# Projecting the queries and keys of head pairs two and three inside the softmax of the pair ahead, in a Mamba and attention hybrid

## The chip, the cores and the metric

The kernel runs as one program on one core of a Trainium2 chip. The metric is the device time of one execution in microseconds (us), the median of three runs. Engines are named as in the profile: PE is TensorE (its weight loads are PEld), DVE is VectorE, ACT is ScalarE, POOL is GpSimd, SP is SyncE, which here only issues DMAs. L725 is line 725 of the kernel before.

## The reference: what is computed

The input holds 8 images of 384 channels and 32 by 32 positions, that is 8 batches of 1024 tokens with 384 channels, all float32. Two layers follow each other for each batch.

Layer 0 norms the channels and runs a Mamba block forward and backward over the tokens: a state of 16 numbers per channel and direction is carried by `h = dA * h + dBu`, and `y = sum over n of h * C`. A depthwise 3x3 convolution is added, and the residual.

Layer 1 is a transformer layer. What matters here is its attention, with 6 heads of 64 channels:

```python
t = x + attention(layernorm(x)); t = t + ffn(layernorm(t))
...
qkv = x @ Wqkv
q, k, v = jnp.split(qkv, 3, axis=2)
...
scores = jnp.einsum('bhqd,bhkd->bhqk', q, k)      # causal mask
attn = jax.nn.softmax(scores, axis=-1)
out = jnp.einsum('bhqk,bhkd->bhqd', attn, v)
return out @ Wproj + bproj
```

The feed-forward layer (384 to 1536 to 384) quantizes by the largest magnitude in groups of batches. It can touch only the first 5 batches, so the kernel computes it for those alone.

## The kernel before: tiles, stages and the order of the work

**Layout.** Channels lie on the 128 partitions in NC = 3 chunks, tokens along the free axis in NH = 2 halves of HB = 512. A head pair is one chunk of 128 channels: head e of pair c sits on partitions 64e to 64e+63.

**Three streams share the engines.** *Before the scan* (`before_scan`): norm, input projection, convolutions, gates, step sizes. *The scan*: 768 units (`units`), each of 2 states of one chunk and half. A unit is a multiply on POOL (`s_first`, L588), two exponentials on ACT (L601), two scans on DVE (L606), a second multiply on POOL (L612), and 8 transposes on PE that add into one PSUM bank (L620). *After the scan*: `attention` and, for five batches, `feed_forward`.

**Who sets the order.** Each stage emits a list of steps, each with a planned cost (2.5 us where none is given). `spread_over` merges lists in proportion to these costs. The end of the kernel function lays all attention and feed-forward steps in a row (`rest`), and deals the scan's slots between them so that a batch's units come before its attention (`due`). Functions are then called in that order. The framework's scheduler turns the calls into one instruction stream per engine: an earlier call has priority, but an instruction whose input or buffer isn't ready at its planned time lets later ones pass. `pin` keeps marked instructions in program order, and `at_once` moves the second head's matmul next to the first head's. [...]

**Attention of one batch** (`attention`, L674):

1. Load the gated scan output, project it (`op`, L695), add to `t`; layernorm of `t`.
2. Project queries and keys, L713 to L732: s = 0 for q and 1 for k, m the head pair, h the token half. Each of these 12 steps takes a PSUM bank, three matmuls of 512 columns (each is two PE instructions in the trace, so 6), and a copy to `q` or `k` by `nc.any`, that is on ACT or DVE, whichever the scheduler finds free.
3. Project the values, 8 steps (L743), then make tile `o`.
4. For each head pair c and query half g, `probabilities` gives one step for each 128 queries and each 512 keys: one score matmul for each head into a bank of tag `s` (L786), mask, row maximum and shift on DVE (L800), exponential with row sum on ACT (L810). There are 12 such steps a pair. `weighted_values`, one half behind, transposes the probabilities on PE (L862), copies them (ACT, L864) and multiplies by the values (L875).
5. Output projection (`ap`, L934).

The last batch's attention runs after all scans, with nothing beside it.

**PSUM.** There are 8 banks, tagged `y` 1, `da` 2, `s` 2, `pt` 2, `av` 1. `bank(name)` without a tag takes `s` and `pt` in turn, so the projections of queries, keys and values rotate over four banks. `s` also serves the scores, `pt` the transposes.

**SBUF.** The pool `big` has six buffers of 128 x 3072 numbers. In attention `t` (normed input), `gy`, `wqk` (weights), `q`, `k`, `v` and `o` come from it. `gy` is free after step 1; in the kernel before, `t` and `wqk` are free after step 3.

Of the kernel before, what the change touches and what calls it, by code (L numbers as in the profile page):

```python
# [20 lines left out]
NC = C // P  # L21
# [33 lines left out]
def kernel(  # L55
# [31 lines left out]
    def btile(name):  # L87
        return big.tile([P, NC, L], F32, name=name, tag="big")
# [10 lines left out]
    def bank(name, tag=None):  # L99
        if tag is None:  # L100
            turn[0] += 1
            tag = ("s", "pt")[turn[0] % 2]
        return ps.tile([P, HB], F32, name=name, tag=tag, bufs=BANKS[tag])

    def half(h):
        return slice(h * HB, (h + 1) * HB)
# [173 lines left out]
    def layernorm(src, name, emit):  # L280

        dst = src
        st = {}
        for h in range(NH):

            @emit.of(6.0)
            def _(h=h):
                mean = mean_of(lambda c: src()[:, c, half(h)], f"mean_{name}_{h}")
                for c in range(NC):
                    nc.vector.tensor_tensor(  # L290
                        dst()[:, c, half(h)], src()[:, c, half(h)], mean, ALU.subtract
                    )
                st[h] = squares(dst(), h, name)

        for h in range(NH):

            @emit.of(6.0)
            def _(h=h):
                var = mean_of(lambda c: st[h][c], f"var_{name}_{h}")
                rstd_of(var, 1)  # L300
                for c in range(NC):
                    nc.vector.tensor_tensor(  # L302
                        dst()[:, c, half(h)], dst()[:, c, half(h)], var, ALU.mult
                    )
# [369 lines left out]
    def attention(b, emit_ffn, emit):  # L674
        st = {}

        @emit
        def _():

            st["t"] = btile(f"t_{b}")  # L680
            st["gy"] = btile(f"gy_{b}")
            for h in range(NH):
                for c in range(NC):
                    load(st["gy"][:, c, half(h)], spilled[b, "gy", c, h])
            for c in range(NC):
                load(st["t"][:, c, :], spilled[b, "t", c])
# [24 lines left out]

        layernorm(lambda: st["t"], f"na_{b}", emit)

        for s in range(2):
            for m in range(NC):
                for h in range(NH):

                    @emit
                    def _(s=s, m=m, h=h):
                        if m == 0 and h == 0:  # L720
                            st["qk"[s]] = btile(f"{'qk'[s]}_{b}")
                        qp = bank(f"qp_{b}_{s}_{m}_{h}")
                        for c in range(NC):
                            o = s * C + m * P
                            nc.tensor.matmul(  # L725
                                out=qp,
                                lhsT=st["wqk"][:, c, o : o + P],
                                rhs=st["xn"][:, c, half(h)],
                                start=(c == 0),
                                stop=(c == NC - 1),  # L730
                            )
                        nc.any.tensor_copy(st["qk"[s]][:, m, half(h)], qp)  # L732
# [176 lines left out]

        waiting = Steps()  # L910
        for c in range(NC):
            for g in range(NH):
                made = Steps()
                probabilities(c, g, made)
                emit.extend(spread_over(made, waiting))
                waiting = Steps()
                weighted_values(c, g, waiting)
        emit.extend(waiting)

        feeds = b < FFN_B  # L920
# [162 lines left out]
    def spread_over(*lists):  # L1083

        keyed = []
        for k, steps in enumerate(lists):
            total, at = sum(us for _, us in steps), 0.0
            for f, us in steps:
                keyed.append(((at + us / 2) / total, k, (f, us)))
                at += us  # L1090
        return [e[2] for e in sorted(keyed, key=lambda e: e[:2])]
# [57 lines left out]
    for i, b in enumerate(ORDER):  # L1149
        if i > 0:  # L1150
            due.append((sum(us for _, us in rest), i * per))
        fed = Steps()
        rest += steps_of(attention, b, fed) if i < B - 1 else []
        if fed and later:
            fed = spread_over(fed, steps_of(before_scan, later.pop(0), ("pt", "pt", "av")))
            fed = [(f, JOINT * us) for f, us in fed]
        rest += fed
# [11 lines left out]
    for _, _, f in sorted(timed, key=lambda e: e[:2]):  # L1169
        f()  # L1170
    run(steps_of(attention, ORDER[-1], Steps()))


# [49 lines left out]
```

## Time and profile before

| | us |
|---|---|
| median of 3 runs (5047.65 to 5053.58) | 5047.94 |
| profiled execution, its own time | 5051.18 |
| its span, first to last instruction | 5049.4 |
| POOL busy / PE busy (modelled) | 3691.4 / 4101.8 |
| DVE busy / ACT busy | 3599.9 / 2721.4 |

In the trace the eight blocks of query and key projections begin at 868, 1550, 2219, 2913, 3611, 3956, 4314 and 4868 us. The first scores of the same attentions follow at 924, 1610, 2284, 2984, 3673, 4013, 4373 and 4915 us, and the last score matmuls begin at 1113, 1800, 2489, 3173, 3864, 4219, 4557 and 5013 us. The last attention starts its first matmul at 4840 us, when POOL has no more work.

How to read it: a group line gives line, engine, operation, what it writes and reads with shapes, count, then busy time, mean ns of one, and the idle time of the engine before it with what ended it. A window line gives a stretch of time and each engine's busy time in it with the number of instructions, then the granted PE clock. A wait line gives who waited for whom, total us, times, longest us. Matmuls are pipelined and their ends are modelled, so the distance between their starts tells more of PE's load than their durations.

### The profile page before, as it was taken

The page shows a single profiled execution, that of the slowest core. Times are in us where ns is not written, and L with a number is a line of the kernel's source. Part 1 is how long each engine was busy: PE and PEld are TensorE (multiplying, and loading weights), DVE is VectorE, ACT ScalarE, POOL GpSimd, SP SyncE. Part 2 cuts the span into 40 slices and gives each one's busy share as a digit, 9 for nine tenths or more (in the row PEclk, how much of TensorE's full clock was granted, in tenths as well). Part 3 has the DMA queues.
Part 4 walks back from the last instruction along what each step waited for, and adds up shares of the span by engine and source line. Part 5 has one row for each costly group of instructions (what it writes and reads, how often), then busy time and mean ns, then how long its engine had stood idle before and what let it go on. Part 6 is the DMA issues. An engine that isn't in the chain of part 4 may idle for free. (4 is left out here: it accounts for less than half of the span.)

```text
span 5049.4 us, 50760 instructions
## 1 busy us (share of the span) xinstructions
PE 4101.8 (81%) x16458; PEld 2191.0 (43%) x16458; DVE 3599.9 (71%) x4780; ACT 2721.4 (54%) x4891; POOL 3691.4 (73%) x1944
## 2 busy tenths in 40 slices
PE   4687787878788888788787888888888978878899
PEld 1243343544434444444443444434444544444444
DVE  6887978667786777876678867678767666666523
ACT  4565665565645656545556446565365455464426
POOL 0578687987669886778876788768788978877710
PEclk7788797989889899888998889898888989989999
DMA  6554646324363334453234633335543334324210
GB/s 230 197 176 158 207 156 226 113 86 144 135 210 117 115 114 163 156 174 125 103 129 143 208 109 127 114 116 191 174 131 115 104 99 141 106 92 132 89 64 26
DMA packets 365010, 696.36 MB, mean 138 GB/s; under 512 B 30104, under 2 KB 88904, under 8 KB 364744
## 3 DMA queue, kind: packets, MB, share of 16 engines
q1 hardware_dynamic: 355232, 676.97, 39.7%
q10 hardware_dynamic: 9512, 16.15, 0.9%
q8 instruction: 130, 2.13, 0.2%
q14 instruction: 136, 1.11, 0.1%
HBM read 527.33 MB, written 165.68 MB: 137 GB/s over the span
## 5 line engine op out<-in xcount | busy, mean ns | idle before, releaser
L588 POOL TENSOR_TENSOR g<-ud,bc 128x1024 f32<-128x1024 f32 x768 | 1839.3, 2395 | 652.0 <-PE y L620 513.1
L612 POOL TENSOR_TENSOR g<-g,bc 128x1024 f32<-128x1024 f32 x768 | 1820.5, 2371 | 228.4 <-DVE g L606 175.6
L601 ACT ACTIVATE da<-dl,amat 128x512 f32<-128x512 f32 x1536 | 1056.1, 691 | 1481.1 <-DVE g L606 1438.6
L606 DVE TENSOR_TENSOR_SCAN g<-da,carry,g 128x512 f32<-128x512 f32 x768 | 957.6, 1271 | 405.7 <-POOL g L588 364.7
L606 DVE TENSOR_TENSOR_SCAN g<-da,g 128x512 f32<-128x512 f32 x768 | 906.4, 1210 | 472.7 <-POOL g L588 439.9
L620 PE MATMUL y<-ident,g 128*128 128x128 f32 x6144 | 932.4, 299 | 270.7 <-POOL g L612 214.6
L620 PEld LDWEIGHTS y<-ident,g 128*128 128x128 f32 x6144 | 772.5, 154 | 729.1 <-POOL g L612 339.9
L786 PE MATMUL s<-k,q 64*128 64x512 f32 (+3 forms) x1152 | 405.1, 610 | 122.9 <-DVE nm L800 111.5
L800 DVE CUSTOM_DVE_ANT_0 pr<-s,cmask 128x512 f32<-128x512 f32 (+3 forms) x576 | 300.6, 545 | 212.6 <-PE s L786 185.8
L810 ACT ACTIVATE pr<-pr,nm 128x512 f32<-128x512 f32 (+3 forms) x576 | 348.8, 606 | 141.7 <-DVE nm L800 139.5
L862 PE MATMUL pt<-ident,pr 128*128 128x128 f32 x1728 | 301.9, 305 | 73.5 <-ACT ptn L864 32.9
L993 PE MATMUL hp<-t,w 128*128 128x512 f32 x720 | 339.4, 617 | 27.1 <-DMA w<-w1s 15.2
L1038 PE MATMUL yp<-h,w 128*128 128x512 f32 x720 | 329.2, 615 | 10.3 <-DMA w<-w2s 5.5
L341 PE MATMUL in<-xn,win 128*128 128x512 f32 x576 | 293.3, 651 | 46.3 <-DVE xc L463 14.8
L862 PEld LDWEIGHTS pt<-ident,pr 128*128 128x128 f32 x1728 | 209.1, 153 | 237.2 <-ACT ptn L864 88.6
L875 PE MATMUL av<-ptn,v 128*64 128x512 f32 (+3 forms) x1152 | 276.6, 563 | 23.9 <-DVE o L889 16.2
L864 ACT COPY ptn<-pt 128x512 f32<-128x512 f32 (+3 forms) x576 | 255.2, 474 | 74.0 <-PE pt L862 72.6
L725 PE MATMUL qp<-t,wqk 128*128 128x512 f32 x576 | 263.9, 608 | 17.5 <-DVE t L302 12.0
L400 DVE SCALAR_TENSOR_TENSOR loc<-xn,vec,loc 128x496 f32<-128x496 f32 (+3 forms) x384 | 260.4, 721 | 24.2 <-ACT loc L389 22.7
L611 POOL COPY carry<-g 128x2 f32<-128x2 f32 x384 | 85.8, 224 | 248.1 <-DVE g L606 248.1
L786 PEld LDWEIGHTS s<-k,q 64*128 64x128 f32 x1152 | 138.4, 208 | 251.8 <-DVE nm L800 187.6
L1038 PEld LDWEIGHTS yp<-h,w 128*128 128x128 f32 x720 | 140.3, 199 | 178.9 <-issue 166.3
(155 smaller groups left out, 4809.8 us busy)
## 6 DMA issues: line engine op xcount, KB each, us to landing
bc<-rows SPq DMA_DIRECT2D x512, 512.0 KB, 4.1
dl<-sdl SPq DMA_DIRECT2D x160, 256.0 KB, 2.9
ud<-sud SPq DMA_DIRECT2D x160, 256.0 KB, 2.7
t<-st SPq DMA_DIRECT2D x63, 512.0 KB, 5.3
su<-u SPq DMA_DIRECT2D x48, 512.0 KB, 3.8
du<-su SPq DMA_DIRECT2D x96, 256.0 KB, 4.5
sdl<-du SPq DMA_DIRECT2D x96, 256.0 KB, 2.4
sud<-du SPq DMA_DIRECT2D x96, 256.0 KB, 2.8
```

Source lines behind the costliest of these rows:

```text
L341: nc.tensor.matmul(out=mp, lhsT=st["win", c][:, k, i, :], rhs=st["xn"][:, k, half(h)], start=(k == 0), stop=(k == NC - 1),)
L588: pin(nc.gpsimd.tensor_tensor(g, ud, sst["bc", 0, u.b, u.part, u.n], ALU.mult))
L601: nc.scalar.activation(da, sst["dl", u.b, u.c, u.part], AF.Exp, scale=amat[:, u.c, n : n + 1])
L606: nc.vector.tensor_tensor_scan(gi[:, ::step], da[:, ::step], gi[:, ::step], first, ALU.mult, ALU.add)
L612: pin(nc.gpsimd.tensor_tensor(g, g, sst["bc", 1, u.b, u.part, u.n], ALU.mult))
L620: nc.tensor.matmul(out=y[:, j, :], lhsT=g[:, i, chunk(j)], rhs=ident, is_transpose=True, start=(u.opens and i == 0 and j == 0), stop=(u.cl ...
L786: mm = nc.tensor.matmul(out=ss[e][:, : k1 - k0], lhsT=st["q"][rows_of(e), c, chunk(qi)], rhs=st["k"][rows_of(e), c, k0:k1], start=True, st ...
L800: nc.vector.tensor_tensor_reduce(out=x, in0=ss[e][:, :w], in1=mask, scale=-1.0, scalar=-MASKED, op0=ALU.add, op1=ALU.min, accum_out=m,)
L810: nc.scalar.activation(x, x, AF.Exp, bias=m, scale=-1.0, accum_out=rs[:, i, e, kb : kb + 1])
L862: nc.tensor.transpose(pt[:, chunk(i)], pr[:, e, chunk(j % QT)], ident)
L993: nc.tensor.matmul(out=hp, lhsT=st["w1"][:, c, chunk(m % 2)], rhs=st["xn"][:, c, half(h)], start=(c == 0), stop=(c == NC - 1),)
L1038: nc.tensor.matmul(out=yp, lhsT=st["w2", k // 6][:, k % 6, :], rhs=st["h", k // NC][:, k % NC, half(h)], start=(k == 0), stop=(k == NF - 1),)
```

## The change

The step list of the query and key projections is split by head pair. Those of pair 0 are emitted where they were. Those of pairs 1 and 2 (8 of the 12 steps) go to lists of their own, and `spread_over` deals the list of pair c+1 evenly among the softmax steps of pair c. Their order among themselves stays: q of both halves, then k of both halves. Steps of pairs 1 and 2 take their PSUM bank from tag `s` alone instead of from `s` and `pt` in turn. Number, size and planned cost of all steps stay as they were.

```diff
+        qk_of = [emit] + [Steps() for m in range(1, NC)]
         for s in range(2):
             for m in range(NC):
                 for h in range(NH):
 
-                    @emit
+                    @qk_of[m]
                     def _(s=s, m=m, h=h):
                         if m == 0 and h == 0:
                             st["qk"[s]] = btile(f"{'qk'[s]}_{b}")
-                        qp = bank(f"qp_{b}_{s}_{m}_{h}")
+                        qp = bank(f"qp_{b}_{s}_{m}_{h}", None if m == 0 else "s")
...
         waiting = Steps()
         for c in range(NC):
+            pair = []
             for g in range(NH):
                 made = Steps()
                 probabilities(c, g, made)
-                emit.extend(spread_over(made, waiting))
+                pair.extend(spread_over(made, waiting))
                 waiting = Steps()
                 weighted_values(c, g, waiting)
+            emit.extend(spread_over(pair, qk_of[c + 1]) if c + 1 < NC else pair)
         emit.extend(waiting)
```

## The prediction, made before the changed kernel ran

> **What bounds the kernel now.** I read the page first, then busy time by stage, then the waits inside one softmax stretch, then the order of time in single steps.
>
> ```profile
> PE 4101.8 (81%) x16458; PEld 2191.0 (43%) x16458; DVE 3599.9 (71%) x4780; ACT 2721.4 (54%) x4891; POOL 3691.4 (73%) x1944
> ...
> L588 POOL TENSOR_TENSOR g<-ud,bc 128x1024 f32<-128x1024 f32 x768 | 1839.3, 2395 | 652.0 <-PE y L620 513.1
> L612 POOL TENSOR_TENSOR g<-g,bc 128x1024 f32<-128x1024 f32 x768 | 1820.5, 2371 | 228.4 <-DVE g L606 175.6
> ...
> L725 PE MATMUL qp<-t,wqk 128*128 128x512 f32 x576 | 263.9, 608 | 17.5 <-DVE t L302 12.0
> ```
>
> No engine is full over the whole span. A scan unit costs POOL 2.395 + 2.371 = 4.77 us, and no unit can pass faster. L725 has 576 instructions: 8 attentions x 12 steps x 6. The stages, three projection blocks first, then the softmax that follows each (busy us of PE, PEld, DVE, ACT, POOL, each with its instruction count, then the granted PE clock):
>
> ```profile
> 868.00:904.00 36.00, 36.00 (x124) 18.73 (x123) 22.61 (x24) 13.74 (x22) 34.81 (x22) 1.00 0.17 50
> 3611.00:3652.00 41.00, 37.71 (x120) 19.06 (x119) 24.67 (x26) 13.89 (x22) 33.84 (x15) 0.96 0.31 103
> 4868.00:4899.00 31.00, 31.00 (x74) 13.75 (x73) 3.15 (x6) 7.69 (x13) 0.00 (x0) 1.00 0.00 0
> ```
> ```profile
> 924.00:1113.00 189.00, 151.51 (x816) 85.62 (x814) 134.96 (x239) 119.32 (x282) 167.44 (x83) 0.87 0.30 103
> 3673.00:3864.00 191.00, 158.93 (x840) 90.10 (x840) 133.41 (x238) 119.81 (x282) 167.70 (x95) 0.86 0.36 117
> 4915.00:5013.00 98.00, 92.55 (x532) 45.06 (x532) 44.52 (x165) 71.85 (x205) 0.00 (x0) 1.00 0.00 1
> ```
>
> Over the seven attentions that have scans beside them, blocks last 36, 38, 45, 48, 41, 36 and 39 us, 283 in sum with POOL busy 257.6 (91%). The softmax stretches last 1354 us with POOL busy 1160.2 (85.7%). So POOL is near its bound in both, a little nearer in the blocks. The last attention has no scans: there its own chain counts alone.
>
> PE is full in the blocks: in the last one 72 instructions start within 30.9 us, 0.43 us apart, a step being 6 x 0.43 = 2.58 us. In softmax, PE only looks full. Where I subtract from the distances between matmul starts what each needs (0.43 us for 512 columns, 0.107 for 128), 77 to 94 of each 184 to 206 us are left over, and 27 of the 117 us of the last attention's (4915 to 5032). The waits within the stretch from 3673 to 3864 us:
>
> ```profile
> DVE g L606 <- POOL g L588: 33.2, 21, 3.4
> POOL g L588 <- PE y L620: 21.4, 12, 3.6
> PEld s L786 <- DVE nm L800: 21.3, 23, 2.8
> ...
> PE s L786 <- DVE nm L800: 12.5, 10, 2.0
> ```
>
> PE waits above all for DVE to empty a score bank, and POOL then waits for transposes queued on PE behind that. In order of time, on PE:
>
> ```profile
> 3707.42 1.09 PE L620 MATMUL y<-ident,g 128*128 128x128 f32 x8
> ...
> 3716.30 0.47 PE L862 MATMUL pt<-ident,pr 128*128 128x128 f32 x1 [2.84 <-ACT ptn L864]
> 3716.56 1.91 PE L620 MATMUL y<-ident,g 128*128 128x128 f32 x8
> ```
>
> After a hole of 2.84 us the same eight transposes take 1.91 us instead of 1.09. And a score step of the last attention:
>
> ```profile
> 4920.81 1.73 PE L786 MATMUL s<-k,q 64*128 64x512 f32 x4 [0.31 <-DVE nm L800]
> ...
> 4921.97 0.69 DVE L800 CUSTOM_DVE_ANT_0 pr<-s,cmask 128x512 f32<-128x512 f32 x1 [0.60 <-PE s L786]
> ...
> 4922.70 0.64 DVE L800 CUSTOM_DVE_ANT_0 pr<-s,cmask 128x512 f32<-128x512 f32 x1
> ```
>
> Both `s` banks are held from 4920.81 to 4923.34, 2.53 us. From first matmul to end of the second reduction the mean over 36 steps is 2.43 us here, 88 of 99 us; in the stretch at 3673 it is 4.14 us, 149 of 194. So the two `s` banks are the tightest thing in softmax after POOL.
>
> **What the Trainium skill says.** *TensorE: Matmul & The Clock Gate*, section "HAM oscillation — how this bites in real kernels": gaps of several us let the PE clock fall to half, and the next matmuls run cold. The trace agrees: 0.86 granted in softmax against 0.96 to 1.00 in blocks, and 1.91 against 1.09 us. *PSUM — Partial Sum Buffer*, "Engine vs sequencer instructions": matmuls start and complete in program order; so transposes of the scan stand behind a waiting score, as the 21.4 us show. *Perfetto Trace Analysis*, "Matmuls": independent groups should rotate through PSUM banks so that emptying one overlaps the next. The block does so with four banks and PE starts every 0.43 us; with two it is not shown.
>
> **The change, part by part.**
>
> *Removed ahead:* 8 steps an attention. In the last one 8 x 2.58 = 20.6 us, all on the path. In the other seven a step costs 283 / 84 = 3.37 us including the scan work within, so 27.0 us each.
>
> *Added inside:* the same 48 PE instructions and 8 copies (0.58 us on ACT, 0.66 on DVE) an attention. No new instruction and no DMA.
>
> *Last attention.* Each step holds an `s` bank for 2.58 + 0.04 (copy lag here) + 0.59 = 3.2 us. It can start when the first score bank is emptied. Of its 2.58 us, about 0.7 lie beside the second reduction and 0.4 in the 0.33 us a step that banks are free (2.76 us period, 99.3 / 36, less 2.43) and similar holes; about 0.3 come back because the next pair of scores gets its second bank only after the copy. So 2.58 - 1.1 + 0.3 = 1.8 us, x 8 = 14.4, against 20.6 removed: **-6**. Bounds: no more than PE's leftover in pairs 0 and 1 (18.7 us by the same subtraction, 4915 to 4991) can be gained; at the full 3.2 us a step it is 25.6 - 20.6 = +5.
>
> *Seven attentions beside scans.* The planned costs don't change, so the moved time takes its units along: 27.0 x 0.91 = 24.6 us of POOL work. Softmax then has 165.7 + 24.6 = 190.3 us of POOL work on average. At its old share that is 190.3 / 0.857 = 222.1 against 193.4 + 27.0 = 220.4: +1.7. At the blocks' 91% it is 209.1: -11.3. I take 87.2%: PE's 84 us of leftover can take in 20.6, the holes that cool the clock shrink, and a projection step asks little of DVE and ACT (one copy), so scans get through beside it; but holes that are waits for an `s` bank can't be filled by a step that needs one. 190.3 / 0.872 = 218.2: -2.2 each, **-16** for seven. Bounds: -79 and, where the banks decide, +35 (rival one).
>
> *Edits costed at nothing.* `t` and `wqk` stay until pair 1 is nearly through: with `q`, `k`, `v`, `o` all six `big` buffers are taken. The trace shows loads into `big` inside softmax (`t2` at 965 us and `x` at 993 us of the first; the next batch's `gy` at 3721). They would come near the start of pair 2 (1041 and 3797 us there), while first needed at 1117 (`ap`), 1166 (`ms`) and 3913 us (`op`); landing takes 5 to 8 us. Cover gone, it is some 8 us at a load. On SP row loads of the scan queue behind such a wait; SP already waits 20 us at a time for POOL in this stretch. First use of pair c+1's keys comes an eighth of a pair, some 8 us, after their last step: covered.
>
> Sum: -6 - 16 = -22. Against the profiled execution's 5051.2 (span 5049.4 and 1.8 around it) that is 5029. The median of the runs lies 3.2 lower: **5026**.
>
> **Rivals.**
>
> *One: the score banks decide (slower).* Beside scans a copy often starts late: 0.3 to 2.5 us after the last matmul in the blocks. A step holds one of two banks for 2.58 + 1.6 + 0.6 = 4.8 us and the next scores need both. Scores of pairs 0 and 1 hold them 101 of 126 us there. For: 77% held, and PE's commonest wait is this one. Against: the other bank still takes one head. It decides from 3.37 us added a step. At 4.0: 0.63 x 8 x 7 = +35, and +5 at the end: 5088.
>
> *Two: the holes are filled.* Softmax reaches the blocks' 91%: -79, and -14 at the end: 4955. For: PE is idle 43% there. Against: its holes come from the bank waits.
>
> *Three: POOL paces both, nothing moves.* +12 (7 x 1.7) - 6 = +6: 5054. It also stands for the scheduler drawing the projections forward, since their inputs are ready, so that the block stays. Against: `s` banks are soon taken.
>
> **How the numbers follow.** Forecast 0.41, own range 5005 to 5037; rival one 0.26, two 0.16, three 0.17. About 10 us (0.2%) is what a measurement can tell from no change. Faster: 0.35 of the forecast, 0.16 of two, 0.03 of three: 0.54. Same: 0.05 + 0.02 (of one) + 0.10 = 0.17. Slower: 0.01 + 0.24 + 0.04 = 0.29. Range 4962 to 5085: it leaves out about half of two and a third of one.
>
> **What would show it.** Right: blocks of 24 instructions at L725; softmax stretches near 218 us with POOL at 87%; the last attention's pairs 0 and 1 some 14 us longer; PE clock in softmax above 0.87. Wrong: score steps holding their banks over 5 us, L786 waiting more for L732 copies than PE had leftover, or POOL's idle before L588 on `y` grown. A reordered schedule in the feed-forward stages, which the change doesn't touch, would break the sum too.

## The result, and the profile after

The changed kernel is slower. Its median is 5089.14 us (four runs, 5087.84 to 5090.45) against 5050.47 us for the kernel before (four runs, 5047.65 to 5053.58); the ratio is 1.008, with an interval of 1.0068 to 1.0092. The profiled execution took 5087.84 us, its span 5086.1 us: 36.7 us more than the span before.

The page of the changed kernel, the lines that answer to those of before:

```profile
PE 4123.5 (81%) x16458; PEld 2194.2 (43%) x16458; DVE 3600.6 (71%) x4785; ACT 2725.2 (54%) x4886; POOL 3691.2 (73%) x1944
...
L588 POOL TENSOR_TENSOR g<-ud,bc 128x1024 f32<-128x1024 f32 x768 | 1835.8, 2390 | 689.8 <-PE y L620 559.0
L612 POOL TENSOR_TENSOR g<-g,bc 128x1024 f32<-128x1024 f32 x768 | 1820.0, 2370 | 227.0 <-DVE g L606 176.7
...
L727 PE MATMUL qp<-t,wqk 128*128 128x512 f32 x576 | 289.7, 644 | 31.9 <-DVE nm L802 18.4
```

The counts of instructions (but for five that went from ACT to DVE), POOL's busy time and the mean of its two operations have stayed. What has grown is idle time: POOL's ahead of L588 for transposes on PE went from 513.1 to 559.0 us, and the projections (L727) now wait for `nm`, the row maximum of a score step, which they never did before.

By stage, in the changed kernel: three blocks from the first projection of queries to the first score, now with four steps of queries and keys ahead of the values, so not of the same extent as the windows of before (length, busy us of PE, PEld, DVE, ACT and POOL, granted PE clock, DMA share, GB/s).

```profile
867.00:899.00 32.00, 31.94 (x129) 19.26 (x127) 20.62 (x23) 11.94 (x19) 31.52 (x20) 1.00 0.15 50
3644.00:3681.00 37.00, 33.71 (x130) 19.99 (x128) 21.83 (x23) 14.50 (x25) 32.74 (x15) 0.95 0.34 114
4901.00:4927.00 26.00, 26.00 (x74) 13.59 (x72) 2.34 (x4) 7.15 (x14) 0.00 (x0) 1.00 0.00 1
```

And the softmax that follows each, from the first score to the last:

```profile
899.00:1121.00 222.00, 183.22 (x892) 100.41 (x892) 149.50 (x253) 127.96 (x294) 189.44 (x97) 0.87 0.30 104
3681.00:3908.00 227.00, 187.26 (x922) 101.12 (x921) 147.79 (x252) 130.04 (x297) 188.06 (x105) 0.88 0.32 104
4927.00:5050.00 123.00, 117.62 (x579) 54.62 (x578) 45.98 (x165) 76.52 (x214) 0.00 (x0) 1.00 0.00 1
```

The first two softmax stretches lasted 189 and 191 us before; they last 222 and 227 now, with POOL busy 85% and 83%, where it was 89% and 88% before. Summed over the attentions, from the start of each stage's first matmul to the start of the next stage's (softmax: to the start of its last score):

| us, seven attentions beside scans | before | after | POOL busy before | POOL busy after |
|---|---|---|---|---|
| queries and keys, up to the first value projection | 288.4 | 102.1 | 259.2 | 90.6 |
| values, up to the first score | 139.8 | 165.1 | 133.4 | 159.6 |
| first to last score | 1356.1 | 1553.9 | 1162.0 | 1304.3 |

The three rows sum to +36.8 us; up to the end of the output projections the seven are 34.9 us longer. The last attention is 4.5 us longer (181.0 against 176.5 us from its first projection to its end): its block is 20.6 us shorter, pairs 0 and 1 are 13.1 and 12.0 us longer. Between the attentions the sum of times moved by 1.3 us. In the seven, pairs 0 and 1 are 115.8 and 81.2 us longer and pair 2 0.9. So what has grown is pairs 0 and 1, and the values by 25.3 us.

Waits inside the softmax stretch from 3681 to 3908 us of the changed kernel (us in total, times, longest):

```profile
DVE g L606 <- POOL g L588: 49.4, 28, 4.7
POOL g L588 <- PE y L620: 37.0, 15, 4.7
DVE pr L802 <- PE s L788: 24.6, 17, 4.6
...
PEld s L788 <- DVE nm L802: 19.0, 23, 3.0
...
PE s L788 <- DVE nm L802: 10.4, 9, 2.7
...
PEld s L788 <- ACT q L734: 4.4, 2, 2.2
```

POOL waits 37.0 us for transposes queued on PE, against 21.4 in the stretch before, and the scores have a new thing to wait for: `q`, the copy that empties a projection's bank. PE in order of time, in the same stretch:

```profile
3686.85 2.84 PE L727 MATMUL qp<-t,wqk 128*128 128x512 f32 x6 [0.86 <-DVE nm L802]
3689.53 0.38 PE L620 MATMUL y<-ident,g 128*128 128x128 f32 x2
3689.84 0.91 PE L788 MATMUL s<-k,q 64*128 64x384 f32 x2
3692.39 1.51 PE L788 MATMUL s<-k,q 64*128 64x384 f32 x2 [1.64 <-ACT q L734]
3693.83 0.47 PE L620 MATMUL y<-ident,g 128*128 128x128 f32 x1
3694.23 2.07 PE L788 MATMUL s<-k,q 64*128 64x512 f32 x2
```

The projection waited for an `s` bank. Then one head's scores started at 3689.84 (`x2`, where one line of `x4` would be both heads), and the other head's only at 3692.39, when the copy had emptied the projection's bank; and the heads stay apart in the next score step. Of the transposes behind the scores, POOL has to wait:

```profile
3700.27 2.34 POOL L588 TENSOR_TENSOR g<-ud,bc 128x1024 f32<-128x1024 f32 x1 [4.75 <-PE y L620]
```

### The profile page after: what moved, and what is told of

It reads as the page before. It is cut to its first block, busy times and chain, and to the rows that moved or that the text cites. A ratio compares the mean times of both kernels' runs of the same rounds, so it can differ in the third digit from the quotient of the medians.

```text
span 5086.1 us, 50774 instructions
## 1 busy us (share of the span) xinstructions
PE 4123.5 (81%) x16458; PEld 2194.2 (43%) x16458; DVE 3600.6 (71%) x4785; ACT 2725.2 (54%) x4886; POOL 3691.2 (73%) x1944
## 5 line engine op out<-in xcount | busy, mean ns | idle before, releaser
L588 POOL TENSOR_TENSOR g<-ud,bc 128x1024 f32<-128x1024 f32 x768 | 1835.8, 2390 | 689.8 <-PE y L620 559.0
L788 PE MATMUL s<-k,q 64*128 64x512 f32 (+3 forms) x1152 | 414.0, 588 | 148.0 <-DVE nm L802 97.3
L727 PE MATMUL qp<-t,wqk 128*128 128x512 f32 x576 | 289.7, 644 | 31.9 <-DVE nm L802 18.4
L611 POOL COPY carry<-g 128x2 f32<-128x2 f32 x384 | 85.7, 223 | 244.2 <-DVE g L606 236.4
```

Of the source, the lines that this page charges most:

```text
L588: pin(nc.gpsimd.tensor_tensor(g, ud, sst["bc", 0, u.b, u.part, u.n], ALU.mult))
L788: mm = nc.tensor.matmul(out=ss[e][:, : k1 - k0], lhsT=st["q"][rows_of(e), c, chunk(qi)], rhs=st["k"][rows_of(e), c, k0:k1], start=True, st ...
```

## The experiments

Each ran beside the kernel before on the same chip, whose medians were 5048.5 to 5051.2 us. Ratios are to it.

| kernel | median us | ratio, interval |
|---|---|---|
| e1_pt_da | 5066.28 | 1.0034 (1.0023 to 1.0046) |
| e2_turns | 5084.43 | 1.0065 (1.0048 to 1.0082) |
| e3_last_alone | 5052.48 | 1.0008 (0.9999 to 1.0017) |
| e4_left_out | 4927.27 | 0.9748 (0.9727 to 0.9769) |
| e5_thirds | 5076.56 | 1.0050 (1.0035 to 1.0064) |
| e6_one_of_three | 5012.49 | 0.9922 (0.9906 to 0.9939) |
| e7_copy_first | 5089.57 | 1.0081 (1.0065 to 1.0097) |
| e8_row | 5026.32 | 0.9948 (0.9933 to 0.9962) |
| f1_twos | 5087.54 | 1.0073 (1.0056 to 1.0090) |
| f2_row_thirds | 5020.37 | 0.9939 (0.9918 to 0.9960) |
| f3_row_s | 5043.06 | 0.9985 (0.9978 to 0.9993) |
| f4_row_midway | 5072.94 | 1.0042 (1.0027 to 1.0057) |

My theory after the result, A below: the score banks decide, as rival one had it. Theory B, against it: the projections' PE time is simply added, whatever the bank, because PE's leftover isn't room for it. A further one, from the later runs: what matters is the place.

**e1_pt_da and e2_turns: which bank.** In the first, moved steps take a bank of the transposes (beside scans) or of the scan (`da`, in the last attention, when no scan needs it); in the second, `s` and `pt` in turn, as in the kernel before.

```diff
-                        qp = bank(f"qp_{b}_{s}_{m}_{h}", None if m == 0 else "s")
+                        tag = "da" if b == ORDER[-1] else "pt"
+                        qp = bank(f"qp_{b}_{s}_{m}_{h}", None if m == 0 else tag)
```
```diff
-                        qp = bank(f"qp_{b}_{s}_{m}_{h}", None if m == 0 else "s")
+                        qp = bank(f"qp_{b}_{s}_{m}_{h}")
```

> The changed kernel with other banks for the moved steps: tag pt in the seven attentions beside scans, tag da in the last one, where both da banks are idle because no scan is left. Theory A (the two s banks decide: the moved steps and the scores queue for them): in the last attention the moved steps no longer compete with anything, so from first projection to last output projection it takes 160 to 170 us instead of 181.0 (176.5 before), and the total falls to about 5050 to 5070. Theory B (PE's in-order stream decides: a step is 2.58 us of PE in one piece, the holes are shorter, so it is added in full whatever its bank): the last attention stays at 178 to 182 us and pairs 0 and 1 still take 12 to 13 us more each; total 5080 to 5095.

> The changed kernel with the moved steps taking s and pt in turn, as the block before did (only the bank choice of the change is undone). Theory A: half of the competition for s is gone, the total falls by 15 to 25 us to about 5065 to 5075. Theory B: 5080 to 5095, the last attention again 178 to 182 us.

Measured: 5066.28 and 5084.43 us. The `s` bank is worth some 23 us (5089.14 - 5066.28), of a loss of 39; with both kinds of bank in turn 5 are won, and e2_turns is where theory B had it. What goes with the bank is seen in the traces. The four instructions of a score step are two for each head. From the first's start to the last's, summed over the score steps of pairs 0 and 1 of the seven attentions, it took 200.5 us before, 257.9 after, 234.3 in e2_turns (whose profiled execution was the fastest of its four) and 208.3 in e1_pt_da. In the list of waits, scores on PE waited 31.7 us for copies of `q` and `k` in the changed kernel (11.6 + 9.6 + 8.0 + 2.5), and not at all in e1_pt_da. The last attention, though, gained next to nothing by the free `da` bank (180.3 us against 181.0 and, before, 176.5), where theory A had 160 to 170; and the seven are still 11.6 us longer than before. So the bank is over half of it, and not all.

**e3_last_alone: the change in the last attention alone.**

```diff
-        qk_of = [emit] + [Steps() for m in range(1, NC)]
+        moved = b == ORDER[-1]
+        qk_of = [emit] + [Steps() if moved else emit for m in range(1, NC)]
...
-            emit.extend(spread_over(pair, qk_of[c + 1]) if c + 1 < NC else pair)
+            emit.extend(spread_over(pair, qk_of[c + 1]) if moved and c + 1 < NC else pair)
```

> The change in the last attention alone; the seven beside scans are as before. From the trace of the changed kernel both theories expect the last attention to take 4 to 5 us more (181.0 against 176.5), so 5053 to 5056. If the loss came from a reordered schedule elsewhere (theory C), this would be at 5045 to 5051, the last attention no longer than before.

Measured: 5052.48 us, ratio 1.0008, an interval that holds no change. The stages resolve what the total doesn't: the block 20.6 us shorter, pairs 0 and 1 13.1 and 12.0 longer, in all 181.0 us against 176.5, to the tenth as in the changed kernel. So the last attention's loss is its own and doesn't come from anything ahead of it.

**e4_left_out: what the eight steps cost where they were.** An edit of the kernel before: the eight steps are left out, and pairs 1 and 2 take their scores from the queries and keys of pair 0.

```diff
-            for m in range(NC):
+            for m in range(1):
...
-                            lhsT=st["q"][rows_of(e), c, chunk(qi)],
-                            rhs=st["k"][rows_of(e), c, k0:k1],
+                            lhsT=st["q"][rows_of(e), 0, chunk(qi)],
+                            rhs=st["k"][rows_of(e), 0, k0:k1],
```

> The kernel before without the eight steps that the change moves: pairs 1 and 2 take their scores from the queries and keys of pair 0, so the eight projections an attention are left out. It prices them: before minus this is what they cost in the block, changed minus this what they cost inside softmax. The last attention should be 20.6 us shorter than before (155.9 us). Theory B: total 23 us less for each of the seven and 20.6 for the last, 5050 - 182 = 4868, so a cost of 182 us in the block and about 221 inside. If POOL paces the attentions beside scans (theory C), their units go elsewhere and the steps are worth little there: 4960 to 5020.

Measured: 4927.27 us, span 4925.2, and so 124 us for 64 steps in the span, 1.9 us each: between the 4868 us of theory B and the 4960 of C. The block is 158.8 us shorter over the seven, about as with the change (160.9), but 31.4 us come back ahead of the blocks (from an attention's first matmul to its first projection of queries), where POOL now has units to work off. A stage beside the scans gives back part of what it saves, since POOL's work stays. The changed kernel is 124 + 37 = 161 us longer than this one, 2.5 us a step. That this is near their PE time of 2.58 says little, since it is a balance: the seven attentions are 184.9 us longer, the last 19.8, and all else 43.8 shorter.

The last attention took 161.2 us, not the 155.9 expected. In 14 us across the end of pair 0 and the start of pair 1 PE was granted half its clock, which the kernel before shows nowhere in its last attention (length, busy us and granted clock as above):

```profile
4805.00:4819.00 14.00, 13.46 (x48) 6.79 (x45) 5.11 (x21) 7.08 (x21) 0.00 (x0) 0.51 0.00 1
```

Pairs 0 and 1 are 5.3 us longer than before for it, and 161.2 - 5.3 is the 155.9. So a few us in a single trace of the last attention can be the clock alone.

**e6_one_of_three: less PE time in each moved step.** Two of the three matmuls of each moved step are left out, so the queries and keys of pairs 1 and 2 are partial sums; bank `s` and the copy stay.

```diff
-                        for c in range(NC):
+                        parts = NC if m == 0 else 1
+                        for c in range(parts):
...
-                                stop=(c == NC - 1),
+                                stop=(c == parts - 1),
```

> The changed kernel with two of the three matmuls of each moved step left out (so queries and keys of pairs 1 and 2 are partial sums); bank s, copy and place are those of the change. Theory B or D (PE's time is added in full): 64 steps x 1.72 us less, pairs 0 and 1 of the last attention grow by 9 to 13 us together instead of 25.1, total 4975 to 5000. Theory A (holding an s bank and waiting for its copy is what costs): the growth stays above 18 us in the last attention and the total above 5040.

Measured: 5012.49 us. In the last attention pairs 0 and 1 grew by 11.3 us instead of 25.1: for each of eight steps 1.72 us of PE time less (4 x 0.43) saved 1.72 us. A step also holds its bank for 1.72 us less; but e1_pt_da, with a bank that nothing else uses there, still had these pairs grow by 23.2 us, so it is PE's time that counts. There the projection's matmuls are added in full, one after the other with all else on PE. What is left at no PE time, (25.1 - 8 x 2.58) / 8, is 0.55 us a step, by extrapolation. In the seven, the three pairs grew by 134.9 instead of 197.8 us: 1.12 us for 1.72, so about a third of PE's time is hidden there.

**e7_copy_first: the copies of the moved steps at high priority.**

```diff
-                        nc.any.tensor_copy(st["qk"[s]][:, m, half(h)], qp)
+                        with tc.high_priority(offset=HURRY if m > 0 else 0):
+                            nc.any.tensor_copy(st["qk"[s]][:, m, half(h)], qp)
```

> The changed kernel with the copies of the moved steps at high priority, so that the s bank is free again sooner (they begin about 2 us after the last matmul beside scans, 0.04 us in the last attention). Theory A, as far as it still holds beside scans (bank pt instead of s brought 23 us): the total falls to 5065 to 5078, all of it in the seven attentions beside scans. Theory B: within 5080 to 5095.

Measured: 5089.57 us, as the changed kernel. But the trace shows that the copies came no sooner: in the seven attentions those of the moved steps began 1.68 us on average after their last matmul, against 1.55 in the changed kernel; in the last attention 0.04 in both. So this run says nothing of late copies, and whether they are part of the bank's price stays open.

**e5_thirds: smaller pieces.** Each moved step is dealt as three steps of one matmul each, so that a piece (0.86 us on PE) may fit more holes; banks as in e1_pt_da.

```diff
-                    @qk_of[m]
-                    def _(s=s, m=m, h=h):
...
+                    for c in range(NC):
+                        qk_of[m](lambda s=s, m=m, h=h, c=c: project(s, m, h, c), 2.5 / NC)
```

> Each moved step is dealt out as three steps of one matmul each (0.86 us of PE instead of 2.58 in one piece), on the banks of the first run (pt beside scans, da in the last attention), so against that run (5066; pairs 0 and 1 of the last attention 10.9 and 12.2 us longer than before) only the grain differs. Theory B in the form 'holes shorter than a step': thirds fit into the holes, pairs 0 and 1 of the last attention grow by 8 to 15 us together instead of 23, its time falls to 165 to 173 us, the total to 5030 to 5050. Theory D (PE's own time is in series with the softmax, the leftover is the latency between dependent steps and nothing placed in an in-order stream reaches it): grain doesn't matter, 20 to 25 us in the last attention, total 5060 to 5070.

Measured: 5076.56 us, above what either theory had. The last attention takes some of the pieces in: its pairs 0 and 1 grew by 17.1 us instead of 23.2 with whole steps in the same bank, and at 173.2 us it is 3.3 shorter than before the change. Beside scans the same is worse than whole steps (+32.1 against +11.6 us). There a bank of the transposes is held from a step's first matmul to its last, with other work dealt between; whether that is what costs wasn't tried alone.

**e8_row, f4_row_midway, f1_twos and f3_row_s: the place.** With banks in turn, the four steps of pair c+1 in a row behind the steps of pair c (e8_row); the same row in the middle of the pair (f4_row_midway); two rows of two steps dealt into the pair (f1_twos); the row behind the pair, in bank `s` alone (f3_row_s).

```diff
-            emit.extend(spread_over(pair, qk_of[c + 1]) if c + 1 < NC else pair)
+            emit.extend(pair + (qk_of[c + 1] if c + 1 < NC else []))
```
```diff
-            emit.extend(spread_over(pair, qk_of[c + 1]) if c + 1 < NC else pair)
+            half_way = len(pair) // 2 if c + 1 < NC else len(pair)
+            row = qk_of[c + 1] if c + 1 < NC else []
+            emit.extend(pair[:half_way] + row + pair[half_way:])
```
```diff
+            if c + 1 < NC:
+                qs = qk_of[c + 1]
+                twos = [(lambda f=qs[x][0], g=qs[x + 1][0]: (f(), g()), 5.0) for x in (0, 2)]
+                emit.extend(spread_over(pair, twos))
+            else:
+                emit.extend(pair)
```

> The four steps of a pair stand in one row behind the softmax steps of the pair ahead instead of being dealt among them, on banks s and pt in turn. Theory B or D: a row costs 4 x 2.58 us as the block did, no more and no less, so the last attention takes 176 to 179 us and the total is 5045 to 5060. If each interruption of the softmax has a price of its own (theory A, banks and lost pairing of the two heads' scores), this is where it shows: the row is 10 to 35 us faster than the change.

> The row of four in the middle of the pair's softmax instead of behind it, banks in turn. One interruption a pair as at the seam: if the number of interruptions decides, 5020 to 5040. If the seam matters (the next pair's scores start there anyway), 5050 to 5085.

> Two rows of two steps (both halves of q, both halves of k) dealt into each pair, banks s and pt in turn: between four single steps a pair (5084) and one row of four behind the pair (5026). If every interruption of the softmax has a price of its own, two interruptions cost half of four: 5045 to 5065. If only the place at the seam between pairs is good, it stays at 5075 to 5090.

> The row of four behind the pair with the change's bank, s alone, so that against the change only the dealing is undone. If the price is of each interruption (second head's scores waiting for a projection's bank), one row meets it once and the bank matters little: 5025 to 5045. If the s bank costs the same per step wherever it stands (it brought 23 us against pt when dealt), 5045 to 5060.

Measured: 5026.32, 5072.94, 5087.54 and 5043.06 us. One row behind the pair is faster than the kernel before (ratio 0.9948, interval 0.9933 to 0.9962); the same row in mid-pair is slower (1.0042, 1.0027 to 1.0057); two rows of two in a pair are no better than four single steps (e2_turns). So it isn't a price for each interruption, which I had come to think: f1_twos and f4_row_midway refute it, and place decides.

What is special behind a pair is seen on PE in the kernel before, at a seam, where one pair's scores end and the next pair's begin; here that of pairs 1 and 2 of the first attention:

```profile
1043.99 1.08 PE L875 MATMUL av<-ptn,v 128*64 128x512 f32 x4
1050.57 1.97 PE L847 MATMUL f<-ident,rs 128*64 128x128 f32 x16 [5.50 <-DVE rs L839]
```

`f` spreads the row sums' factors, which the weighted values of the half before need, and `rs` comes at the end of that half's scores, maxima, exponentials and DVE's queue. PE stood still for 5.50 us with everything queued behind it. With the row ahead of it, PE in e8_row at the seam of pairs 0 and 1 of the first attention (the first line below holds two of the row's four steps):

```profile
956.05 5.32 PE L727 MATMUL qp<-t,wqk 128*128 128x512 f32 x12
961.20 1.04 PE L620 MATMUL y<-ident,g 128*128 128x128 f32 x8
...
968.14 1.06 PE L620 MATMUL y<-ident,g 128*128 128x128 f32 x8 [1.70 <-ACT yt L635]
969.13 1.09 PE L849 MATMUL f<-ident,rs 128*64 128x128 f32 x16
```

PE no longer waits for `rs`; a hole of 1.70 us for the scan's `yt` is what stands ahead of `f`. The waits of the whole program, of before, changed kernel, e8_row and f4_row_midway in this order:

```profile
POOL g L588 <- PE y L620: 513.1, 211, 10.7
...
PE f L847 <- DVE rs L839: 62.2, 16, 7.1
```
```profile
POOL g L588 <- PE y L620: 559.0, 230, 9.1
...
PE f L849 <- DVE rs L841: 46.7, 13, 7.1
```
```profile
POOL g L588 <- PE y L620: 487.6, 212, 10.7
...
PE f L849 <- DVE rs L841: 27.5, 7, 7.1
```
```profile
POOL g L588 <- PE y L620: 539.1, 207, 10.9
...
PE f L849 <- DVE rs L841: 62.1, 17, 7.1
```

The row behind the pair takes PE's wait for `rs` from 62.2 to 27.5 us, and POOL's wait for transposes below that of before; the row in mid-pair leaves the first as it was (62.1) and POOL waits longer. It is the place that is hit: of the 62.2 us, 35.1 lie just after the two seams of the seven attentions, where the rows stand in e8_row, and 27.1 behind pair 2, where no row does. In e8_row none is left at the seams, and 27.5 us behind pair 2; in f4_row_midway it is 34.9 and 27.3. By stage, e8_row shows pairs 0 and 1, which hold the rows, longer by 97.3 and 66.9 us over the seven and pair 2 shorter by 31.5. The wait for `rs` in pair 2 was 14.8 of these; what makes up the rest isn't divided. In the changed kernel pair 2 stays (+0.9). f3_row_s against e8_row gives the bank's price at this place, 17 us. Even so the row in bank `s` is a little faster than the kernel before (0.9985, 0.9978 to 0.9993); that is inside the range expected for a price of each interruption, which the other two runs refute.

**f2_row_thirds: both gains.** The row behind the pair in the seven attentions, thirds in bank `da` in the last.

```diff
-            emit.extend(spread_over(pair, qk_of[c + 1]) if c + 1 < NC else pair)
+            ahead = qk_of[c + 1] if c + 1 < NC else []
+            last = b == ORDER[-1] and ahead
+            emit.extend(spread_over(pair, ahead) if last else pair + ahead)
```

> One row behind the pair in the seven attentions beside scans, as in the run at 5026, and thirds on the idle da banks in the last attention, as in the run whose last attention took 173.2 us. If the two effects are separate, as the stages say, the last attention is 8 us shorter than with the row (181.3) and the total 5014 to 5022, below the kernel before and every other version.

Measured: 5020.37 us, 0.9939 (0.9918 to 0.9960), faster than both kernels. Against e8_row the totals don't resolve a difference. In the stages the last attention is 8 us shorter (173.2 against 181.3), but most of that can be the clock: e8_row's trace has two stretches at half clock there, f2_row_thirds none.

```profile
4931.00:4941.00 10.00, 9.84 (x19) 3.64 (x18) 4.49 (x17) 4.12 (x12) 0.00 (x0) 0.50 0.00 0
4982.00:4989.00 7.00, 6.92 (x23) 3.15 (x20) 3.68 (x12) 3.42 (x10) 0.00 (x0) 0.51 0.24 74
```

f3_row_s, with the same place of the steps and 3.4 us at half clock, took 176.4 us. So the thirds are worth some 3 us in the last attention, as in e5_thirds, and not 8.

## Why the prediction was wrong

The forecast was 22 us faster, the measurement 39 slower; of the 63 us between 5026 and 5089, 2.5 come from the median of before, 5047.94 with three runs and 5050.47 with four. By the prediction's own steps:

- **Removed ahead: right.** The last block became shorter by 20.6 us, as worked out. In the seven, queries and keys became shorter by 186.3 us (288.4 to 102.1), 3.33 us a step for 3.37 predicted. What the prediction didn't see: of the 168.6 us of POOL's work that left them, 26.1 went to the value projections, which grew by 25.3 us, and 142.3 to softmax, not all of it.
- **"I take 87.2%": wrong, and this step failed.** POOL was busy 83.9% of the longer softmax (1304.3 of 1553.9 us), not 87.2% and not the old 85.7%. At 87.2% the same work would have taken 1496 us. The 58 us between make up the error of the seven attentions, some 52 us (-16 predicted, which is -15.4 by its own factors, and +36.8 measured); what the values took up and what softmax was spared nearly cancel. The reason given was that PE's leftover could take in the moved PE time. On balance it did not. By the same subtraction, from first projection to last score, PE's leftover in the seven was 632 us before and 660 after. If a third of the moved time is hidden there, as e6_one_of_three shows, new holes came beside it. The leftover is holes at certain places of a chain of waits (for a bank, for `rs`). The Trainium skill says in *PSUM — Partial Sum Buffer*, "Engine vs sequencer instructions", that matmuls start and complete in program order, and the 5.50 us for `rs` with PE's work queued behind it agree: a step dealt to another place can't go into such a hole, and what is behind it comes later.
- **"About 1.1 us of each step lies beside": wrong.** In the last attention it was nothing, as e6_one_of_three measured. Pairs 0 and 1 grew by 25.1 us, not 14.4: 8 x 2.58 of PE time and 8 x 0.55 besides. PE's leftover there was some 16 us before and 18 after (the 18.7 of the prediction reach to 4991 us, 14 us into pair 2). The bound named (full cost of 3.2 us a step, +5 in all) is what came.
- **The banks.** That a step which needs an `s` bank can't fill holes that are waits for one was said, and then priced too low. Own price, by e1_pt_da: 23 us. A score step holds its banks no longer than before (4.14 to 4.18 us in the fifth attention's softmax, 2.43 to 2.41 in the last's), so the sign named for this, over 5 us, did not come. A moved projection held its bank for 5.3 us on average in the seven. What goes with the price is that the two heads' scores come apart and wait for copies; that this is how the time is lost isn't shown. In e5_thirds the sum from first to last score matmul is only 167.5 us, less than before, and it is slower than e1_pt_da.
- **Clock and POOL's idle.** The granted clock of the seven softmax stretches rose from 0.86 to 0.89 on average, as foreseen, and softmax became longer all the same. POOL's idle before L588 on `y` grew by 46 us: the sign named for the forecast being wrong.
- **Edits costed at nothing.** SyncE now waits 21.2 us for projections before it issues loads (of `t` and `gy`), as it never did before; no engine's wait for those loads grew by it.

Rival one named 5088 and 5089 came. Its size is right; its cause is right in part. It put the whole price on the banks, with late copies in it, which no run put to the test. The banks are 23 of the 39 us; the rest is, by e6_one_of_three, PE time that found no hole where it was dealt. That its number came so near is in part luck. Rival two, the holes filled, is refuted for the dealing as it was written. POOL at the forecast's share came with e8_row: 87.5% (1301.9 of 1488.7 us), by the place of the steps and not by the dealing; that e8_row also took the forecast's 5026 us is chance. Rival three, no effect, is refuted.

What stays open: by which way an `s` bank costs its 23 us, late copies among them; why single steps in banks of the transposes (e1_pt_da) still cost 11.6 us in the seven, while thirds there cost more; whether the spells at half clock in the last attention come from the order of the steps, since each kernel left one trace; and whether more buffers for the scan would let it run ahead over the longer holes wasn't tried.

## What to carry to other kernels

PE's idle share in this softmax wasn't room. Look for the places where an engine's stream stands still longest and what for, and try independent work just ahead of those instructions: here a row of four steps at such a place gained 25 us, and the same row in mid-pair lost 22. Work dealt evenly was added in full in the attention without scans and to about two thirds beside them. Give such work banks of another group than the one that the stretch waits for: that was worth 23 us when dealt and 17 in a row.

## What the runs showed of the hardware

Two score matmuls of 64 rows each, one for each head, cost together as much as one if they are next to each other. PE in the last attention of the changed kernel, at full clock:

```profile
4972.85 0.70 PE L788 MATMUL s<-k,q 64*128 64x256 f32 x4
...
4998.01 0.70 PE L788 MATMUL s<-k,q 64*128 64x256 f32 x2 [0.78 <-DVE nm L802]
```

Both heads, four instructions of 256 columns, take 0.70 us; one head alone takes 0.70 as well. So heads that come apart cost PE a whole score matmul more. In the softmax beside scans, where half the clock was granted from 3692.6 to 3702.8 us, it is the same at 512 columns: 2.07 us for one head (the line at 3694.23 above) and 2.08 for both.

```profile
3700.11 2.08 PE L788 MATMUL s<-k,q 64*128 64x512 f32 x4
```

At half clock PE's work takes nearly twice as long. Eight transposes in e4_left_out, within the stretch shown there and behind it:

```profile
4810.93 1.97 PE L862 MATMUL pt<-ident,pr 128*128 128x128 f32 x8
...
4821.45 1.09 PE L862 MATMUL pt<-ident,pr 128*128 128x128 f32 x8
```
